# Scores from the edge features, computed in the first of two message phases

## The chip, the cores and the metric

The kernel runs on one core of a Trainium2 chip. The time is the device time of one execution in microseconds, shown as the median of several runs. A profiled execution gives, besides, when each instruction ran on each engine: PE (matrix products), DVE (vector work), ACT (activations and copies), POOL (here mostly gathers from memory, issued as indirect DMAs), and SP, which only issues DMAs.

## The reference, cut to what matters

The reference is a chain of four graph layers and four feed-forward layers over 3125 nodes with 256 features and 50000 edges sorted by destination. The change touches two graph layers.

Layer 0 adds up, for each node, transformed rows of the sources of its edges; layer 1 adds up products of embedding rows with a linear map of 64 edge features:

```
msg = transformed[rel_type, src] * norm                       # layer 0
W = (edge_feats @ W_dist + b_dist) * cut[:, None]             # layer 1
msgs = embed_table[node_z][senders] * W
agg = segment_sum(msgs, receivers)
```

Layer 2 is an attention over edges, whose logit has a part that depends on the edge features alone:

```
concat_z = concatenate([z[edge_src], z[edge_dst], w], axis=-1)   # w: edge features, 64 wide
e = leaky_relu(concat_z @ W_att.T)[:, 0]
```

The last 64 weights of `W_att`, times `w`, give one number for each edge: the "score from the edge features". It depends on inputs only, so a kernel can compute it at any time before layer 2.

## The kernel before, in words

The kernel starts with three pieces of work that share one hand-written order (`manual_schedule`: every engine executes its instructions in the order in which the program issues them).

**The first phase** (`stage_one`, L777 to 903). A short lead computes 24 `chunk`s. A chunk (L618) is one 128x512 piece of the table `tabt` of node rows, transformed for 16 relations; every fourth chunk SP writes 1 MB of it (L630). Then a loop over k from 0 to 195 (L880) does layer 1's sums. Every second step, `four` (L861) multiplies edge features by `wd` on PE into the PSUM tiles `pw` (three of them, filled with the bias by ACT, L858) and DVE multiplies the result by gathered embedding rows into `mt` (L871). Each step also does one more chunk until all 200 are done (k = 175), and lets POOL gather rows for a pair twelve steps ahead (`fetch_rows`, L810). Once in four steps come a feature load on SP (L851), the one-hot matrix on DVE (L825, L827), and `add_up` (L829): PE sums a group of edges, ACT copies it to `p_out` (L837), SP writes it out (L839 and L842). Four steps are called a round of the first phase here. In the remaining room, L900 takes one step of a background generator `bg` for each odd k. There `bg` is `ranks` (L1180), which finds where each node's edges begin; it has 25 yields.

**The second phase** (`stage_two`, L908 to 1176). Its loop has 49 groups of eight slots, 392 slots. Eight slots are a round of the second phase. Each round gathers eight tiles of `tabt` rows with POOL and adds up a group for layer 0 with `add_up`. As soon as a block of nodes has its sums, a `Flow` (L1109) takes two node tiles through the feed-forward layer 0, layer 1's output and the inputs of layer 2, spread over the next slots; three flows overlap, and each fetches its sums by gathers `p` on POOL (L927). Every second slot (`BG_EVERY`, L109) `between` (L1143) takes a step of a second background generator: first `by_degree` (L1273), which sorts the nodes by degree (37 yields), then `records` (L1352). From slot 60, zeros for later tables are written by SP in odd slots (L713).

`records` does four products for the attention weights (L1358), then the scores: 100 steps, each with one load of four edges for each of 125 partitions (`part`, L1367), three steps ahead of its use, a multiplication by the weights `a3` (L1377) and a sum over the 64 features into `rect` (L1378). Then it writes the pairs (source, score) to memory (L1384), reads them back in windows by node (`window`, L1389, 25 gathers on POOL), and masks them into `srcI` and `ewF` (L1401 to 1407).

Scores have four buffers (`b_at`), in the pool `sh` that both phases share. A score load's issue on SP thus waits for the sum of the step before, and it stands in SP's order behind whatever was issued earlier.

Of the kernel before, what the change touches and what calls it, by code (L numbers as in the profile page):

```python
# [9 lines left out]
F32 = mybir.dt.float32  # L10
# [3 lines left out]
OP = mybir.AluOpType  # L14
# [5 lines left out]
P = 128  # L20
# [4 lines left out]
D = 256  # L25
E = 50000
EP = 125
ET = 400
# [84 lines left out]
def tile_gnn_ffn(ctx: ExitStack, tc: tile.TileContext, a: dict, out: bass.AP):  # L113
# [7 lines left out]
    @contextmanager  # L121
    def psums(**bufs):
        with tc.tile_pool(name="psum", bufs=1, space=PSUM) as p:
            before = dict(banks)
            banks["pool"], banks["bufs"] = p, bufs
            yield
            banks.update(before)

    def ps(tag, shape):
        return banks["pool"].tile(shape, F32, name=tag, tag=tag, bufs=banks["bufs"][tag])  # L130
# [11 lines left out]
    def bcast(src, n, pool, name):  # L142

        t = pool.tile([P, n], F32, name=name)
        nc.sync.dma_start(t, bass.AP(tensor=src.tensor, offset=src.offset, ap=[[0, P], [1, n]]))
        return t
# [38 lines left out]
    wfa = per.tile([P, 2, ZW], F32, name="wfa")  # L185
# [198 lines left out]
    wb = w1st.enter_context(tc.tile_pool(name="wb", bufs=1))  # L384
    stt = nc.vector.scalar_tensor_tensor
# [22 lines left out]
    junk = pp.tile([EP, ET], F32, name="fl_junk")  # L408
# [48 lines left out]
    with tc.If(uns > 0):  # L457

        rec = dram.tile([E, RW], F32, name="rec")
        with tc.tile_pool(name="srt", bufs=1) as ep, tc.tile_pool(name="srt2", bufs=2) as eb, \  # L460
# [23 lines left out]
            for b in range(ET // BT):  # L484
# [10 lines left out]
                junk = eb.tile([EP, P], F32, name="s_junk")  # L495
                for i in range(BT):
# [5 lines left out]
                                                   op1=OP.mult, accum_out=before[:, 0, i : i + 1])  # L502
                    nc.vector.scalar_tensor_tensor(junk[:, :EP], row[:EP, e], dstf[:, j : j + 1], lower[:EP, :EP],
                                                   op0=OP.is_equal, op1=OP.mult, accum_out=before[:, 1, i : i + 1])
# [37 lines left out]
    def tp(width):  # L542
        return flatb()[:, :width]
# [233 lines left out]
    def stage_one():  # L777
# [24 lines left out]

        sh = w1st.enter_context(tc.tile_pool(name="sh", bufs=2))
        w = {}
        bg, loads = ranks(sh), late_weights(sh, w)
        pairs = NW // 2
        rows, feats, hots = {}, {}, {}
        at = {"rows": 0, "feats": 0, "chunk": LEAD}
# [35 lines left out]
        with tc.tile_pool(name="ea", bufs=1) as ea, psums(t=2, pw=3, agg=1, w=2):  # L844

            def fetch_feats():
                g = at["feats"]
                if g < NG:
                    at["feats"] += 1
                    feats[g] = ea.tile([P, 4 * P], F32, name="f", bufs=F_BUFS)  # L850
                    nc.sync.dma_start(feats[g], a["attr_2"][:, 4 * P * g : 4 * P * (g + 1)])  # L851

            mults, biased = {}, []

            def bias():

                pw = ps("pw", [P, 2, D])
                nc.scalar.copy(pw, bd.unsqueeze(1).to_broadcast([P, 2, D]))  # L858
                biased.append(pw)

            def four(k):  # L861

                g = k // 4
                for h in range(2):
                    for b in range(2):
                        o, half = (k % 4 + h) * P, slice(64 * b, 64 * b + 64)
                        nc.tensor.matmul(biased[b][:, h, :], feats[g][half, o : o + P], wd[half, :], start=False,
                                         stop=True, skip_group_check=True)
                for b in range(2):
                    m = mults[k + b] = ea.tile([P, 2, D], F32, name="mt", bufs=8)  # L870
                    nc.vector.tensor_tensor(m, biased.pop(0), rows.pop(k + b), op=OP.mult)  # L871

            for _ in range(F_BUFS - 1):
                fetch_feats()
            for _ in range(G_PAIRS):
                fetch_rows()
            make_hots(0, cutW)
            bias()
            bias()
            for k in range(pairs):  # L880
                g = k // 4
                if k % 4 == 0:
                    fetch_feats()
                if k % 2 == 0:
                    four(k)
                if at["chunk"] == 8 * NT:
                    next(loads, None)
                else:
                    chunk(next(chunks), ea)
                    at["chunk"] += 1  # L890
                    next(norms, None)
                if k % 2 == 0 and k + 2 < pairs:
                    bias()
                    bias()
                fetch_rows()
                if k % 4 == 1 and g:
                    add_up(g - 1, [mults.pop(4 * (g - 1) + j) for j in range(4)], part1)
                if k % 4 == 2:
                    make_hots(g + 1, cutW)
                if k % 2:  # L900
                    next(bg, None)
            add_up(NG - 1, [mults.pop(4 * (NG - 1) + j) for j in range(4)], part1)
            assert next(bg, None) is None and next(loads, None) is None
# [274 lines left out]
    begI_of = []  # L1178
# [92 lines left out]
    kept = {}  # L1271
# [77 lines left out]
        nc.vector.tensor_copy(begI, begR)  # L1349
        begI_of.append(begI)  # L1350

    def records(sh, w):  # L1352

        begI = begI_of[0]
        for i in range(2):
            for k in range(2):
                junk = sh.tile([P, D], F32, name="w_junk", bufs=1)
                stt(junk, wfa[:, k, :D], 1.0, w[f"aw{i}"], op0=OP.mult, op1=OP.mult, accum_out=wfa[:, k, D + i : D + i + 1])  # L1358
            yield

        a3 = bcast(a["L2_gnn_W_att"][:, 2 * D :], 64, wb, "b_a3")
        attr = a["edge_attr_64"].rearrange("(p t) d -> p t d", p=EP)
        rect = wb.tile([EP, ET, 2], F32, name="b_rect")
        nc.vector.tensor_copy(rect[:, :, 0], srcf)
        ats = {}

        def part(b):  # L1367
            if b < ET:
                ats[b] = sh.tile([EP, AB, 64], F32, name="b_at", bufs=4)
                nc.sync.dma_start(ats[b], attr[:, b : b + AB, :])  # L1370

        for b in range(0, 3 * AB, AB):
            part(b)
            yield
        for b in range(0, ET, AB):
            old = ats.pop(b)
            nc.vector.tensor_tensor(old, old, a3[:EP].unsqueeze(1).to_broadcast([EP, AB, 64]), op=OP.mult)  # L1377
            nc.vector.tensor_reduce(rect[:, b : b + AB, 1], old, axis=AX.X, op=OP.add)  # L1378
            part(b + 3 * AB)
            yield  # L1380

        nc.vector.tensor_sub(ews, ews, rect[:, :, 1])
        stt(rect[:, :, 1], ews, unsorted[:EP, :], rect[:, :, 1], op0=OP.mult, op1=OP.add)
        nc.sync.dma_start(rec2[:E, :].rearrange("(p t) w -> p t w", p=EP), rect)  # L1384
        yield

        ws = {}

        def window(t):  # L1389
            ws[t] = sh.tile([P, 32, 2], F32, name="k_w", bufs=3)  # L1390
            gather(ws[t][:, : RND[t], :].rearrange("p r w -> p (r w)"), rec2, begI[:, t : t + 1])

        window(0)
        window(1)
        for t in range(NT):
            n, s, w = RND[t], slice(OFF[t], OFF[t + 1]), ws.pop(t)
            if t + 2 < NT:
                window(t + 2)
            yield
            mk = sh.tile([P, 32], F32, name="k_mk")  # L1400
            nc.vector.tensor_scalar(mk[:, :n], iota_f[:, :n], degR[:, t : t + 1], None, op0=OP.is_lt)  # L1401
            sf = sh.tile([P, 32], F32, name="k_sf")
            stt(sf[:, :n], w[:, :n, 0], idF[:, t : t + 1], mk[:, :n], op0=OP.subtract, op1=OP.mult)
            nc.vector.tensor_scalar(srcI[:, s], sf[:, :n], idF[:, t : t + 1], None, op0=OP.add)
            nc.vector.tensor_tensor(ewF[:, s], w[:, :n, 1], mk[:, :n], op=OP.mult)
            nc.vector.tensor_scalar(mk[:, :n], mk[:, :n], BIG, -BIG, op0=OP.mult, op1=OP.add)
            nc.vector.tensor_add(ewF[:, s], ewF[:, s], mk[:, :n])

        for t in range(NT):
            nc.gpsimd.memset(rndF[:, t : t + 1], float(RND[t]))  # L1410
        mo = wb.tile([P, NT], F32, name="k_mo")
        mx = wb.tile([P, 1], F32, name="k_mx")
        nc.vector.tensor_sub(mo, degR, rndF)
        nc.vector.tensor_reduce(mx, mo, axis=AX.X, op=OP.max)
        pk = tp(P)
        nc.tensor.transpose(pk[:1], mx, ident)
        m0 = wb.tile([1, 1], F32, name="k_m0")
        nc.vector.tensor_reduce(m0, pk[:1], axis=AX.X, op=OP.max)
        nc.vector.tensor_scalar_max(m0, m0, 0.0)
        nc.vector.tensor_copy(more_i, m0)  # L1420
        yield

    stage_one()
    order.close()
    w1st.close()
# [23 lines left out]
    with tc.tile_pool(name="f1", bufs=1) as fp, tc.tile_pool(name="f1b", bufs=2) as fb, psums(mm=3, y=3, tp=2):  # L1449
# [17 lines left out]
        junk = fp.tile([P, NT], F32, name="f_junk")  # L1467
# [12 lines left out]
        for sh in range(28, -1, -4):  # L1480
# [3 lines left out]
            if sh < 28:  # L1484
# [8 lines left out]
                                    accum_out=c1)  # L1493
# [16 lines left out]
        with tc.If(tie > 0):  # L1510

            with tc.tile_pool(name="f1t", bufs=1) as tp_:
# [12 lines left out]
                for t in range(NT):  # L1525
                    w_ = wtb[:, t : t + 1]
                    nc.vector.tensor_scalar(less, row[:, :N], w_, None, op0=OP.is_gt, op1=OP.add,
                                            accum_out=cn[:, t, 0:1])
# [1010 lines left out]
```

## Time and profile before

| what | value |
|---|---|
| median of 3 runs | 3418.66 us (3414.97 to 3419.67) |
| the profiled execution | 3418.41 us, span 3416.7 us |
| mean granted clock of PE | 0.787 |
| busy: PE, DVE, ACT, POOL | 2240.7, 1678.1, 898.8, 1999.7 us |
| DMA: score loads | 100 of 125.0 KB, issued from 771.7 to 1103.6 us |
| DMA: table writes of the first phase | 50 of 1024.0 KB |
| DMA: feature loads, sum writes | 49 of 256.0 KB, 98 of 256.0 KB |

Busy time is a sum over the whole program. The two phases with which this text deals lie in the first 1320 us or so: layer 1's sums run from 106 to 650 us, the second phase's loop from there to about 1315 us. What limits one of them can be read only from windows of that time, and from the order of an engine's instructions: an engine that waits keeps all that stands behind it waiting. A number such as "4.66 <-ACT p_out L837" behind an instruction is the idle time of its engine before it, and what ended that.

### The profile page before, as it was taken

The numbers are of one execution on the slowest core, as the hardware profiler recorded it, in microseconds if no ns is written. First come the engines' busy times: TensorE is split into PE (matmuls) and PEld (weight loads), VectorE is DVE, ScalarE is ACT, GpSimd is POOL, SyncE is SP. The second block draws the span as 40 slices with busy tenths as digits, with TensorE's granted clock in tenths as the row PEclk, the third lists the DMA queues.
The fourth block names the chain that finished last, engine by engine and source line by source line (L and its number), as shares of the span: only waits on it lengthen the run. The fifth ranks groups of instructions, "written<-read, shape, count | busy, mean of one in ns | idle before, by whom it ended". The sixth has DMA issues, their size and how long they took to land. (4 is left out here: it accounts for less than half of the span.)

```text
span 3416.7 us, 36379 instructions
## 1 busy us (share of the span) xinstructions
PE 2240.7 (66%) x10325; PEld 1557.2 (46%) x10325; DVE 1678.1 (49%) x6067; ACT 898.8 (26%) x2016; POOL 1999.7 (59%) x2265
## 2 busy tenths in 40 slices
PE   4689999777888779849322585877711212259993
PEld 1334444345666557637211373756511112237672
DVE  2343333557787766533365565566723333366211
ACT  1334545312233223312110131323300000024341
POOL 3677777766666671011577777764467777732433
PEclk9889999758999889959655696888755555559997
DMA  7577777857775452031243585876233333325562
GB/s 238 183 229 245 254 253 251 255 135 228 235 235 177 111 144 80 31 130 50 80 111 104 158 262 176 266 257 188 95 90 106 105 105 106 105 76 165 166 217 81
DMA packets 246803, 553.65 MB, mean 162 GB/s; under 512 B 49584, under 2 KB 131251, under 8 KB 240174
## 3 DMA queue, kind: packets, MB, share of 16 engines
q0 software_dynamic: 103296, 283.74, 27.8%
q1 hardware_dynamic: 137624, 261.43, 23.6%
q10 hardware_dynamic: 5654, 5.88, 0.6%
q8 instruction: 90, 1.47, 0.2%
q14 instruction: 139, 1.14, 0.1%
HBM read 394.00 MB, written 156.83 MB: 161 GB/s over the span
## 5 line engine op out<-in xcount | busy, mean ns | idle before, releaser
L153 POOL DMA_INDIRECT g<-tabe,e_src x392 | 371.2, 947 | 196.2 <-issue 97.2
L153 POOL DMA_INDIRECT g_rows<-tab,srcI x413 | 402.4, 974 | 126.9 <-issue 104.8
L153 POOL DMA_INDIRECT g_row<-tab,srcI x413 | 390.6, 946 | 131.6 <-issue 119.8
L153 POOL DMA_INDIRECT g<-tabt,e_code x392 | 377.9, 964 | 151.1 <-issue 79.5
L625 PE MATMUL t<-w_big,n_xt 128*128 128x512 f32 x800 | 378.7, 619 | 0.5 <-ACT n_xt L613 0.5
L2386 DVE TENSOR_TENSOR ACC<-ACC,g_row 128x256 f32<-128x256 f32 x413 | 175.8, 426 | 341.4 <-DMA g_row<-tab,srcI 341.3
L1638 PE MATMUL tp<-ident,ACC 128*128 128x128 f32 x50 | 16.6, 435 | 420.4 <-DVE ACC L2386 420.4
L871 DVE TENSOR_TENSOR mt<-pw,g 128x512 f32<-128x512 f32 x196 | 126.7, 686 | 257.0 <-ACT p_out L837 145.6
L1970 PE MATMUL mm<-ro_xt,ro_w 128*128 128x192 f32 (+3 forms) x928 | 232.2, 401 | 28.9 <-ACT ro_h L2051 21.4
L1974 PE MATMUL y<-ro_w,ro_h 128*96 128x256 f32 (+2 forms) x1040 | 243.7, 388 | 1.5 <-ACT ro_h L2051 1.5
L625 PEld LDWEIGHTS t<-w_big,n_xt 128*128 128x128 f32 x800 | 148.8, 195 | 185.7 <-issue 184.1
L1018 PE MATMUL w<-xt,w_big 128*128 128x256 f32 (+1 forms) x832 | 214.2, 399 | 0.0
L2261 DVE SCALAR_TENSOR_TENSOR ACC<-g_rows,g_e,ACC 128x256 f32<-128x256 f32 x413 | 201.2, 487 | 13.4
L1970 PEld LDWEIGHTS mm<-ro_xt,ro_w 128*128 128x128 f32 x928 | 170.2, 205 | 73.3 <-ACT ro_h L2051 27.4
L157 POOL DMA_INDIRECT xg<-XX,ro_pos x100 | 100.8, 1008 | 174.8 <-issue 72.5
L1638 PEld LDWEIGHTS tp<-ident,ACC 128*128 128x128 f32 x50 | 7.2, 203 | 428.1 <-issue 353.2
L1974 PEld LDWEIGHTS y<-ro_w,ro_h 128*96 128x96 f32 (+2 forms) x1040 | 181.7, 180 | 44.1 <-ACT ro_h L2051 1.9
L1027 PE MATMUL w<-w_big,b_h 128*128 128x256 f32 x800 | 198.9, 387 | 1.6 <-DVE n_x L1029 1.6
L628 ACT COPY n_tst<-t 128x512 f32<-128x512 f32 x200 | 117.2, 586 | 266.7 <-PE t L625 239.7
L153 POOL DMA_INDIRECT ro_g<-yg,ro_back x100 | 99.4, 994 | 137.3 <-issue 67.4
L1018 PEld LDWEIGHTS w<-xt,w_big 128*128 128x128 f32 x832 | 162.7, 209 | 27.2 <-issue 4.9
L1027 PEld LDWEIGHTS w<-w_big,b_h 128*128 128x128 f32 x800 | 154.0, 195 | 24.2 <-DVE n_x L1029 2.0
(579 smaller groups left out, 4349.8 us busy)
## 6 DMA issues: line engine op xcount, KB each, us to landing
tabt<-n_tst SPq DMA_DIRECT2D x50, 1024.0 KB
ro_w<-in_L_ffn_blocks SPq DMA_DIRECT2D x58, 514.0 KB
ro_w<-in_L_ffn_blocks SPq DMA_DIRECT2D x58, 512.0 KB
part<-p_out SPq DMA_DIRECT2D x98, 256.0 KB
xg<-zero SPq DMA_DIRECT2D x78, 200.0 KB
f<-in_attr SPq DMA_DIRECT2D x49, 256.0 KB
b_at<-in_edge_attr SPq DMA_DIRECT2D x100, 125.0 KB
tabr<-v SPq DMA_DIRECT2D x11, 770.0 KB
```

The source lines that it names most:

```text
L153: return nc.gpsimd.indirect_dma_start(out=dst, out_offset=None, in_=table, in_offset=bass.IndirectOffsetOnAxis(ap=idx, axis=0))
L157: return nc.gpsimd.indirect_dma_start(out=table, out_offset=bass.IndirectOffsetOnAxis(ap=idx, axis=0), in_=src, in_offset=None)
L625: nc.tensor.matmul(pt, xt_of[t][:, k, :], wrel[:, k, 2 * i : 2 * i + 2, :].rearrange("p r d -> p (r d)"), start=(k == 0), stop=(k == 1))
L628: nc.scalar.copy(stage[0][:, o : o + 2 * D], pt)
L871: nc.vector.tensor_tensor(m, biased.pop(0), rows.pop(k + b), op=OP.mult)
L1018: nc.tensor.matmul(ph, w["01"][:, e, k, i * P : (i + 1) * P], xt[:, k, : n * h], start=(k == 0), stop=(k == 1))
L1027: nc.tensor.matmul(py, last[:, k, i * h : (i + 1) * h], w["02"][:, e - 1, k, :], start=(k == 0), stop=(k == 1))
L1638: nc.tensor.transpose(pt[:, k, :m], src[:, k * P : (k + 1) * P], ident[:m, :m])
L1970: nc.tensor.matmul(ph, w[:, o : o + P], xt[:, k, :], start=(k == 0), stop=(k == 1))
L1974: nc.tensor.matmul(py, h[:, i, s], w[:, i * D : (i + 1) * D], start=(i == 0), stop=(i == self.fc - 1))
L2261: stt(u, g[:, r, :D], e[:, r0 + r : r0 + r + 1], u, op0=OP.mult, op1=OP.add)
L2386: nc.vector.tensor_tensor(u, u, rows.pop(r), op=OP.max)
```

## The change

The part of `records` that computes the scores becomes a generator of its own, `scores`, with one yield for each of the three first loads and one for each of the 100 steps. It is appended to `ranks` in the first phase's background. Because the first phase would take too few steps with one for every odd k, from k = 56 on each k takes one. `records` finds the scores ready in `kept["rect"]`.

```diff
-        bg, loads = ranks(sh), late_weights(sh, w)
+        bg, loads = (step for part in (ranks(sh), scores(sh)) for step in part), late_weights(sh, w)
...
-                if k % 2:
+                if k % 2 or k >= 56:
                     next(bg, None)
...
-    def records(sh, w):
-
-        begI = begI_of[0]
-        for i in range(2):
-            for k in range(2):
-                junk = sh.tile([P, D], F32, name="w_junk", bufs=1)
-                stt(junk, wfa[:, k, :D], 1.0, w[f"aw{i}"], op0=OP.mult, op1=OP.mult, accum_out=wfa[:, k, D + i : D + i + 1])
-            yield
+    def scores(sh):
 
         a3 = bcast(a["L2_gnn_W_att"][:, 2 * D :], 64, wb, "b_a3")
         attr = a["edge_attr_64"].rearrange("(p t) d -> p t d", p=EP)
-        rect = wb.tile([EP, ET, 2], F32, name="b_rect")
+        rect = kept["rect"] = wb.tile([EP, ET, 2], F32, name="b_rect")
         nc.vector.tensor_copy(rect[:, :, 0], srcf)
         ats = {}
...
             nc.vector.tensor_tensor(old, old, a3[:EP].unsqueeze(1).to_broadcast([EP, AB, 64]), op=OP.mult)
             nc.vector.tensor_reduce(rect[:, b : b + AB, 1], old, axis=AX.X, op=OP.add)
             part(b + 3 * AB)
+            yield
+
+    def records(sh, w):
+
+        begI, rect = begI_of[0], kept["rect"]
+        for i in range(2):
+            for k in range(2):
+                junk = sh.tile([P, D], F32, name="w_junk", bufs=1)
+                stt(junk, wfa[:, k, :D], 1.0, w[f"aw{i}"], op0=OP.mult, op1=OP.mult, accum_out=wfa[:, k, D + i : D + i + 1])
             yield
 
         nc.vector.tensor_sub(ews, ews, rect[:, :, 1])
```

So the 100 loads and 200 DVE instructions of the scores are issued between k = 51 and k = 155 of the first phase, and `records`, which followed them, runs in the second phase right behind `by_degree`.

## The prediction

> **What bounds the kernel now.** I read the busy times by stretch first, then the timeline of one round of the first phase, the tile of the score loads, the ends of the second phase's rounds, and last the trace's DMA packets. The stretches (columns: busy us and instructions of PE, PEld, DVE, ACT and POOL, then granted clock, DMA share, GB/s):
>
> ```profile
> 300.00:600.00 300.00, 300.00 (x1396) 139.32 (x1392) 95.41 (x172) 151.16 (x285) 215.43 (x228) 1.00 0.77 252
> 840.00:1028.00 188.00, 162.19 (x867) 122.08 (x860) 147.69 (x551) 59.02 (x136) 121.54 (x126) 0.91 0.73 234
> 1028.00:1110.00 82.00, 73.00 (x377) 55.66 (x376) 63.60 (x240) 27.74 (x62) 53.17 (x55) 0.92 0.57 175
> 1121.00:1245.00 124.00, 89.24 (x437) 66.43 (x438) 82.94 (x380) 31.38 (x73) 87.87 (x115) 0.85 0.43 117
> 1245.00:1315.00 70.00, 64.57 (x367) 50.19 (x367) 46.31 (x196) 25.84 (x61) 40.02 (x42) 0.98 0.50 144
> ```
>
> The first phase (row one) is bound by PE: never idle at clock 1.00, DVE 32% busy. The second phase (rows two to five) has no full engine; DVE is 78% busy where the scores run. DVE in a round of the first phase (four steps k):
>
> ```profile
> 406.16 1.29 DVE L871 TENSOR_TENSOR mt<-pw,g 128x512 f32<-128x512 f32 x2 [4.66 <-ACT p_out L837]
> 407.37 0.42 DVE L825 TENSOR_TENSOR s<-iota_f,e_low 128x256 f32<-128x256 f32 x1
> 407.81 0.43 DVE L827 TENSOR_TENSOR s<-s,e_cut 128x256 f32<-128x256 f32 x1
> 410.86 1.29 DVE L871 TENSOR_TENSOR mt<-pw,g 128x512 f32<-128x512 f32 x2 [2.61 <-PE pw L867]
> 416.58 1.29 DVE L871 TENSOR_TENSOR mt<-pw,g 128x512 f32<-128x512 f32 x2 [4.44 <-ACT p_out L837]
> ```
>
> The round is 416.58 - 406.16 = 10.42 us, with 4.44 + 2.61 = 7.05 us in which DVE waits for PE. The score step that moves:
>
> ```profile
> L1370 SPq DMA_DIRECT2D b_at<-in_edge_attr x100: 257/275/2237, 771.7 to 1103.6; - x100
> L1377 DVE TENSOR_TENSOR b_at<-b_at,b_a x100: 391/418/487, 782.5 to 1115.9; 125x256 f32<-125x256 f32 x100
> L1378 DVE TENSOR_REDUCE b_rect<-b_at x100: 419/420/422, 783.1 to 1116.3; 125x4 f32<-125x256 f32 x100
> ```
>
> And ends of the second phase's rounds (eight slots; round 9 ends at 775.95, 35 at 1121.53, 42 at 1244.72, 48 at 1314.55):
>
> ```profile
> 775.95 0.59 ACT L837 COPY p_out<-agg 128x512 f32<-128x512 f32 x1 [0.68 <-PE agg L834]
> ...
> 1121.53 0.56 ACT L837 COPY p_out<-agg 128x512 f32<-128x512 f32 x1
> ...
> 1244.72 0.59 ACT L837 COPY p_out<-agg 128x512 f32<-128x512 f32 x1 [0.74 <-PE agg L834]
> ...
> 1314.55 0.59 ACT L837 COPY p_out<-agg 128x512 f32<-128x512 f32 x1 [0.73 <-PE agg L834]
> ```
>
> So a round takes 345.6/26 = 13.3 us beside scores, 123.2/7 = 17.6 us beside the windows (the gathers k_w), and 69.8/6 = 11.64 us with neither.
>
> **DMA engines.** The trace counts a DMA's semaphore up engine by engine. Of each zero write between 900 and 1000 us eleven engines report first, close together (most within 4 us), a twelfth is in between, and four come late, mostly 7 to 10 us after the issue. The score loads (125 partitions) get only about five such reports after landing begins, the sum writes of L839 (4x32 rows) four. So these DMAs do not use all engines, and the slow ones are the same few. Their load, with the median packet times of the trace (1024 B 46 ns, 1600 B 67, 2048 B 84, 4096 B 159, 8192 B 309), score packets spread over five engines, sum writes over four, all else over sixteen: in stretches of 40 us from 776 to 1096 it is 1.02, 0.94, 1.00, 1.03, 1.00, 1.00, 0.94, 0.89 of the time. These engines were full for 240 us while the mean DMA share stood at 0.73.
>
> **Removed from the second phase.** 100 steps of 0.418 + 0.420 us on DVE, one in two slots (3.35 us a round), 100 SP issues of 0.275 us, 12.8 MB of loads, and a 0.36 us copy. Records, its 25 window gathers on POOL and 25 memsets come 204 slots sooner: rounds 10 to 16, beside the early flows. Windows cost POOL four more gathers a round: (8 + 1 + 4) x 1.25 us (a gather 0.95 plus 0.30 to the next) = 16.3, near the 17.6 seen, so I keep 7 x 17.6 = 123.2 us, which also holds the 11.3 us that POOL waits for the records' write. Rounds 9 to 48 last 1314.55 - 775.95 = 538.6 us. After: 123.2 + 32 x 11.64 = 496 us, a gain of 43; I take 40 for meeting early flows. Bounds: 32 rounds at POOL's own 9 x 1.25 = 11.25 us gain 55; at 12.4 us, if PE's chains through DVE and ACT stay the limit, 19. The zero writes that now run beside clean rounds cost nothing: the rounds beside scores were no slower with them (13.3 against 13.5 us), and without scores the few engines have room.
>
> **Added to the first phase.** Score step i runs at k = 56 + i, one a step until k = 155: 25 rounds, with three loads ahead at k = 51, 53, 55. The b_rect copy and the a3 broadcast load come once, under the same idle.
> DVE: 4 x 0.84 = 3.35 us into 7.05 us idle. Two steps behind one mt leave 4.44 - 1.68 = 2.8 us, the two behind the one-hots 2.61 - 1.68 = 0.9: nothing, if the loads are there. The cover is PE's ten microseconds of work.
> SP: four issues more (1.1 us) beside four others (1.7 us) in 10.42 us: nothing. They stand in order behind the table write (waits for ACT n_tst L628) and the sum write (waits for p_out), so a load leaves when its round has come that far.
> POOL: nothing is issued; a gather waits for mt to free its rows, twelve pairs ahead, so its lateness is covered.
> The few DMA engines, per round now: table write 8 x 309 = 2.47 us, feature load 8 x 84 = 0.67, eight gathers 16 x 159 = 2.54, sum write 32 x 84 = 2.69, small ones 0.1: 8.5 of 10.42 us. The scores add 4 x 25 x 46 ns = 4.6 us. Together 13.1 us. At most 1.03 full was seen, so a round cannot be shorter than 12.7; at 0.99 it is 13.2. DVE runs in order: a score's multiply that waits for its load holds the next mt, ACT's bias copies wait for mt (three pw banks), PE's pw for those. Three loads ahead bridge no lasting shortage. So 25 x (13.2 - 10.42) = 70 us. Bounds (PE is full, so no gain is to be had here): nothing, as for the mean load (252 GB/s + 4 x 128,000 B/10.42 us = 301 GB/s, and the trace held 350 GB/s at 10 to 30 us); and with the mean packet times of 300 to 600 us (queueing included: 10.4 + 5.05 = 15.4 us) 125 us. I take 70, nearest to the stretch from 776 to 1028, which has these same score loads, sum writes and gathers on full engines.
> PE's clock: 0.91 at 86% busy in row two. PE's 10.42 us at 0.85 are 12.3, still under 13.2: nothing more; it is in the upper bound.
>
> Rule against row: the Trainium skill, DMA: Bandwidth & Descriptors, section Bandwidth, gives about 358 GB/s per core as the limit for transfers with HBM. By it 301 GB/s fit, the 70 us vanish, and the sum would be 3418.4 - 40 = 3378. The row speaks against taking one limit for all sixteen engines: 234 GB/s went with few engines full.
>
> **Sum** against the profiled execution (3418.4 us, span 3416.7, within 0.3 us of the median 3418.66): + 70 - 40 = + 30, so 3448 us.
>
> **Rivals.**
> A, the loads are hidden and the change gains. For it: 7.05 us of idle DVE, a mean share of 0.77, peaks of 350 GB/s, a lead of three steps (7.8 us). Against: score loads that DVE waited for had been issued 8.3 to 11.8 us before. It decides if the round stays under 10.42 + 40/25 = 12.0 us, a load of 13.1/12.0 = 1.09 on the few engines, where 1.03 was the most seen. Cost 0 to 20, gain 40 to 55: 3363 to 3398.
> B, cost and gain cancel: round at 11.8 to 12.3 us with a gain of 40 to 45: 3408 to 3425.
> C, worse than counted: loads late in bursts, PE falling to half clock in the gaps (0.64 at 71% busy between 700 and 800), rounds of 14.3 to 15.4 us: + 97 to 125, less 20 to 40: 3475 to 3523.
> That the scores stay where they were is excluded: the changed program issues all 100 between the first phase's mt.
>
> **How the numbers follow.** Few engines full 0.66 (own range 3428 to 3475), A 0.18, B 0.07, C 0.09. A measurement tells 0.2% (6.8 us) from nothing: faster 0.18, same 0.07, slower 0.75. The range from 3392 to 3490 leaves out most of A's better half and C's worse half.
>
> **What would show it.** Right: between about 300 and 620 us rounds near 13.2 us instead of 10.42, PE under 85% busy, DVE's score multiply (now L1370) waiting for b_at for 60 us or more; the first phase's last round some 70 us later; then rounds of 17.6 us from round 10 and under 12 us from round 17, p_out of round 48 near 1345 us; all after that as before. Wrong: rounds of 10.4 us there (A), or rounds of 13 us in the second phase without scores, which would mean that DVE was not what they shared.

## The result and the profile after

The changed kernel takes 3443.09 us (median of 6 runs, 3440.36 to 3444.44) beside 3419.16 us for the kernel before in the same comparison: 1.0070 of it, 95% interval 1.0057 to 1.0083, so it is slower by 24 us. Its profiled execution took 3440.36 us, with a span of 3438.6. Some of the later comparisons ran about a fifth slower as a whole, the kernel before included (4051 to 4131 us at a granted clock of 0.74 to 0.75, instead of some 3419 us at 0.78 to 0.79); why is open, and no reading rests on them.

Busy times by stretch of the changed kernel (columns as before: PE, PEld, DVE, ACT, POOL, granted clock, DMA share, GB/s):

```profile
360.00:600.00 240.00, 217.74 (x885) 98.29 (x886) 117.54 (x252) 94.43 (x181) 137.44 (x146) 0.98 0.70 240
...
1000.00:1100.00 100.00, 92.65 (x518) 72.15 (x516) 66.53 (x271) 36.10 (x83) 74.55 (x78) 0.98 0.75 233
```

In the first phase PE is no longer without gaps, and DMA moves *less* per microsecond than before (240 against 252 GB/s), although the score loads came in. In the second phase DVE has gone from 78% to 67%. The ends of rounds show what that did to each phase. First rounds 14 and 38 of the first phase in the kernel before:

```profile
320.83 0.59 ACT L837 COPY p_out<-agg 128x512 f32<-128x512 f32 x1 [0.39 <-PE agg L834]
...
573.57 0.59 ACT L837 COPY p_out<-agg 128x512 f32<-128x512 f32 x1 [0.39 <-PE agg L834]
```

Then the changed kernel (rounds 14, 19, 38 and the last, 48, of the first phase, then 9, 16, 35 and 48 of the second):

```profile
320.38 0.60 ACT L837 COPY p_out<-agg 128x512 f32<-128x512 f32 x1
...
385.99 0.57 ACT L837 COPY p_out<-agg 128x512 f32<-128x512 f32 x1
...
638.51 0.60 ACT L837 COPY p_out<-agg 128x512 f32<-128x512 f32 x1
...
724.49 0.59 ACT L837 COPY p_out<-agg 128x512 f32<-128x512 f32 x1 [10.74 <-DMA part<-p_out]
...
841.90 0.59 ACT L837 COPY p_out<-agg 128x512 f32<-128x512 f32 x1 [0.68 <-DMA xg<-zero]
...
962.74 0.59 ACT L837 COPY p_out<-agg 128x512 f32<-128x512 f32 x1 [1.60 <-PE agg L834]
...
1184.12 0.56 ACT L837 COPY p_out<-agg 128x512 f32<-128x512 f32 x1
...
1337.40 0.59 ACT L837 COPY p_out<-agg 128x512 f32<-128x512 f32 x1 [0.97 <-PE agg L834]
```

| stretch | before | after |
|---|---|---|
| a round of the first phase (14 to 38) | 252.74/24 = 10.53 us | 318.13/24 = 13.26 us |
| end of the first phase's last round | 660.1 us | 724.5 us |
| second phase, rounds 9 to 48 | 538.6 us | 495.5 us |
| rounds with windows (35 to 42 before, 9 to 16 after) | 17.6 us | 17.3 us |
| rounds 16 to 35 | 13.4 us (with scores) | 11.65 us (nothing beside) |
| end of round 48 | 1314.6 us | 1337.4 us |

The first phase loses 64 to 66 us and the second gains 43. After the second phase's loop the kernels run alike: the spans differ by 21.9 us, the loops' ends by 22.9.

How the loss reaches PE is told by the changed kernel's waits between 360 and 600 us (us in total, times, longest):

```profile
DVE b_at L1370 <- DMA b_at<-in_edge_attr: 118.0, 71, 3.2
POOL g L153 <- DVE mt L871: 69.3, 36, 3.6
...
ACT pw L858 <- DVE mt L871: 59.9, 34, 3.5
PEld pw L867 <- ACT pw L858: 48.9, 51, 2.1
```

DVE's multiply waits for its load, mt stands behind it, ACT's bias copy waits for mt, PE's pw for the copy. Over the whole run DVE waited 164.7 us for score loads, in 98 of 100 steps; before, in the second phase, 17.5 us in 9. The same in one round of DVE's timeline:

```profile
428.29 0.42 DVE L1370 TENSOR_TENSOR b_at<-b_at,b_a 125x256 f32<-125x256 f32 x1 [2.95 <-DMA b_at<-in_edge_attr]
428.75 0.42 DVE L1371 TENSOR_REDUCE b_rect<-b_at 125x4 f32<-125x256 f32 x1
429.42 0.43 DVE L1370 TENSOR_TENSOR b_at<-b_at,b_a 125x256 f32<-125x256 f32 x1 [0.25 <-DMA b_at<-in_edge_attr]
429.88 0.42 DVE L1371 TENSOR_REDUCE b_rect<-b_at 125x4 f32<-125x256 f32 x1
430.22 1.28 DVE L871 TENSOR_TENSOR mt<-pw,g 128x512 f32<-128x512 f32 x2
```

mt now follows a late score step without a gap; before, it had waited 2.6 to 4.7 us for PE.

### The profile page after: what moved, and what is told of

Same layout as the page of the kernel before. It is cut to its first block, busy times and chain, and to the rows that moved or that the text cites. A ratio compares the mean times of both kernels' runs of the same rounds, so it can differ in the third digit from the quotient of the medians.

```text
span 3438.6 us, 36411 instructions
## 1 busy us (share of the span) xinstructions
PE 2254.0 (66%) x10325; PEld 1559.6 (45%) x10325; DVE 1687.1 (49%) x6067; ACT 895.3 (26%) x2016; POOL 1997.9 (58%) x2265
## 5 line engine op out<-in xcount | busy, mean ns | idle before, releaser
L2263 DVE SCALAR_TENSOR_TENSOR ACC<-g_rows,g_e,ACC 128x256 f32<-128x256 f32 x413 | 201.2, 487 | 13.4
L867 PE MATMUL pw<-w_d,f 64*128 64x256 f32 x784 | 156.0, 423 | 78.3 <-ACT pw L858 66.4
L1018 PE MATMUL w<-xt,w_big 128*128 128x256 f32 (+1 forms) x832 | 204.3, 386 | 0.0
```

The lines of the kernel that those rows point to most:

```text
L1018: nc.tensor.matmul(ph, w["01"][:, e, k, i * P : (i + 1) * P], xt[:, k, : n * h], start=(k == 0), stop=(k == 1))
L2263: stt(u, g[:, r, :D], e[:, r0 + r : r0 + r + 1], u, op0=OP.mult, op1=OP.add)
```

## The experiments

The theory: a load of 125 partitions runs on five DMA engines and the sum write of L839 on four of the same, so these engines are full while the rest are not. Its rivals: the lead of three loads is too short for a longer latency; SP cannot issue that much, or the DMA system as a whole is full. And for the second phase: was its gain from DVE's relief, or from the engines'?

**Spread the score loads** (changed kernel):

```diff
-                nc.sync.dma_start(ats[b], attr[:, b : b + AB, :])
+                for lo, hi in ((0, 112), (112, EP)):
+                    nc.sync.dma_start(ats[b][lo:hi], attr[lo:hi, b : b + AB, :])
```

> Each score load is issued as two, of 112 and of 13 partitions, so that its packets can be spread over 16 and 13 engines instead of five; bytes, packets, lead and DVE work stay. Few full engines (my theory): the fullest engine then has 8.5 + 4 x 8 x 0.046 = 10.0 us of packets in a round of the first phase, PE's 10.42 us bind again, rounds of 10.4 to 10.8 us, total 3443 - 65 = 3378 us (3370 to 3386). SP's issue or the DMA system as a whole is the limit (after the change SP's issues last up to 3.7 us): four more issues in a round and the same bytes, rounds of 13.3 us or more, total 3443 or more. The lead is too short for the latency: rounds shorten only as far as each load lands sooner, somewhere between 10.5 and 13.

Measured: 3382.72 us beside 3421.55, ratio 0.9881 (0.9855 to 0.9907). Rounds of the first phase take 252.75/24 = 10.53 us, the number of the kernel before. Its rounds 14 and 38, and its stretch from 360 to 600 us:

```profile
320.51 0.59 ACT L837 COPY p_out<-agg 128x512 f32<-128x512 f32 x1 [0.39 <-PE agg L834]
...
573.26 0.59 ACT L837 COPY p_out<-agg 128x512 f32<-128x512 f32 x1 [0.39 <-PE agg L834]
```

```profile
360.00:600.00 240.00, 240.00 (x1125) 111.37 (x1123) 140.19 (x296) 121.73 (x230) 175.35 (x183) 1.00 0.88 294
```

PE is without gaps again, with the same bytes to move, one issue more for each step, and DMA at 294 GB/s. So neither SP's issues nor the whole of DMA were the limit. What the scores cost in the first phase is nothing, once their loads are spread, and this kernel keeps the second phase's gain (494.2 us for rounds 9 to 48). It is faster than both kernels.

**Spread the sum writes instead** (changed kernel; the score loads stay on five engines):

```diff
-            nc.sync.dma_start(v[:, :8, :].rearrange("l (j h) d -> j l (h d)", h=2), o)
+            for j in range(4):
+                nc.sync.dma_start(v[:, 2 * j : 2 * j + 2, :].rearrange("l h d -> l (h d)"), o[32 * j : 32 * j + 32, :])
```

> The score loads stay as the change has them; instead the sum write of L839 (4 x 32 rows) is issued as four writes of 32 rows, which can use 16 engines each. Few full engines: 8.5 - 2.69 + 0.67 + 4.6 = 11.1 us on the fullest engines, rounds of 11.0 to 11.5 us where the scores are, total near 3443 - 25 x 2.1 = 3391 us. SP's issue or all of the DMA system: three more issues in a round, 13.3 us or more, 3443 or more. Lead too short: about 13.3 us, since the score loads are issued as before.

Measured: 3402.53 us (one run), rounds of 275.78/24 = 11.49 us (rounds 14 and 38 shown):

```profile
321.87 0.59 ACT L837 COPY p_out<-agg 128x512 f32<-128x512 f32 x1 [0.39 <-PE agg L834]
...
597.65 0.60 ACT L837 COPY p_out<-agg 128x512 f32<-128x512 f32 x1
```

The score loads were issued as in the changed kernel, with as short a lead, and yet 1.8 us of each round went. The account by packets said 11.1; the fullest engines were at 0.96 by it. The total is above the 3391 expected, chiefly because the round came out at the upper end.

**A longer lead** (changed kernel):

```diff
-                ats[b] = sh.tile([EP, AB, 64], F32, name="b_at", bufs=4)
+                ats[b] = sh.tile([EP, AB, 64], F32, name="b_at", bufs=7)
...
-        for b in range(0, 3 * AB, AB):
+        for b in range(0, 6 * AB, AB):
             part(b)
-            yield
+            if b % (2 * AB):
+                yield
...
-            part(b + 3 * AB)
+            part(b + 6 * AB)
```

> The score loads run six steps ahead (seven buffers) instead of three. Lead too short for the latency: the loads are in time, rounds of 10.4 to 11 us, total 3378 to 3392 us. Few full engines, or SP's issue: a longer lead bridges no lasting shortage, rounds stay at 13.0 to 13.4 us, total 3436 to 3446 us.

Measured: 3442.88 us (one run), rounds of 13.34 us; DVE waits 165.5 us for loads, as with a lead of three (164.7). So it is a shortage of throughput, not of lead.

**The same spread in the kernel before** (the first edit, at its L1370):

> The kernel before, with its score loads (in the second phase) issued as two of 112 and 13 partitions. It asks what held the rounds of the second phase beside the scores at 13.3 us. Few full engines there too (1.00 full by packet times from 776 to 1028 us): rounds of 11.7 to 12.3 us, total 3419 - 26 x 1.3 = 3385 us (3379 to 3394). DVE's 3.35 us of score work a round in the chains of PE and ACT: rounds stay at 13.3 us, total 3415 to 3421 us.

Measured: 3411.72 us, ratio 0.9970 (0.9959 to 0.9981). Neither expectation held fully. The early rounds, 9 to 16, shorten from 12.9 to 11.8 us, but rounds 16 to 35 stay at 13.48 us (13.43 before):

```profile
777.01 0.59 ACT L837 COPY p_out<-agg 128x512 f32<-128x512 f32 x1 [0.68 <-PE agg L834]
...
859.85 0.59 ACT L837 COPY p_out<-agg 128x512 f32<-128x512 f32 x1 [1.60 <-PE agg L834]
...
1116.01 0.56 ACT L837 COPY p_out<-agg 128x512 f32<-128x512 f32 x1
```

So in the second phase the full engines cost some 7.5 us in the early rounds, and something else held the later ones.

**The two halves of a score step, each in another phase** (changed kernel: the loads stay in the first phase and nothing reads them; the DVE instructions go to the second phase, where they were, and multiply the first four edges each time, so the scores are other numbers). The edit is cut at each "...":

```diff
@@ scores
-            nc.vector.tensor_tensor(old, old, a3[:EP]..., op=OP.mult)
-            nc.vector.tensor_reduce(rect[:, b : b + AB, 1], old, axis=AX.X, op=OP.add)
             part(b + 3 * AB)
...
@@ records, before the records are written
+        only = wb.tile([EP, AB, 64], F32, name="b_only")
...
+        for b in range(0, ET, AB):
+            old = sh.tile([EP, AB, 64], F32, name="b_at", bufs=4)
+            nc.vector.tensor_tensor(old, only, a3[:EP]..., op=OP.mult)
+            nc.vector.tensor_reduce(rect[:, b : b + AB, 1], old, axis=AX.X, op=OP.add)
+            yield
```

> One kernel that takes the score step apart and puts its halves into different phases: the 100 score loads in the first phase, on five engines, read by nothing, and the 200 DVE instructions in the second phase, where the kernel before had them, multiplying the first four edges each time (so the scores are other numbers). First phase, rounds 14 to 38: if DVE's wait for a load in front of mt carries the loads' lateness to PE, 10.5 us; if the full engines and SP's order do so by themselves, 12.7 to 13.3 us (I expect this). Second phase, rounds 16 to 35: if DVE's instructions made the rounds beside the scores 13.4 us, 13.0 to 13.5 us (I expect this); if the loads did, 11.6 to 12.2 us. Total by my expectations 3419 + 60 = 3479 us (3465 to 3490); by the other two 3419 - 35 = 3384 us.

> The same kernel once more (score loads in the first phase, read by nothing; DVE's score instructions in the second, on the first four edges), beside a kernel before that takes some 3420 us again, if this chip gives that. First phase, rounds 14 to 38: 10.5 us if only DVE's wait carries the loads' lateness to PE, 12.7 to 13.3 us if the full engines and SP's order do so by themselves (I expect this). Second phase, rounds 16 to 35: 13.0 to 13.5 us if DVE's instructions made the rounds beside the scores (I expect this), 11.6 to 12.2 us if the loads did. Total by my expectations 3465 to 3490 us.

The first of these took 4066.78 us beside 4070.74 for the kernel before, and nothing is read from it. The second took 3472.04 us (one run) beside 3419.15. Rounds 14 to 38 of the first phase: 308.36/24 = 12.85 us. Rounds 16 to 35 of the second: 13.40 us. Both as expected. First the waits, between 360 and 600 us, then the ends of rounds 14, 19, 38 and 48 of the first phase and of rounds 9, 16, 35 and 48 of the second:

```profile
ACT n_tst L628 <- DMA tabt<-n_tst: 83.4, 15, 7.5
...
DVE mt L871 <- PE pw L867: 64.9, 18, 5.4
```

```profile
319.61 0.59 ACT L837 COPY p_out<-agg 128x512 f32<-128x512 f32 x1 [0.39 <-PE agg L834]
...
372.87 0.58 ACT L837 COPY p_out<-agg 128x512 f32<-128x512 f32 x1
...
627.97 0.61 ACT L837 COPY p_out<-agg 128x512 f32<-128x512 f32 x1
...
723.69 0.59 ACT L837 COPY p_out<-agg 128x512 f32<-128x512 f32 x1 [11.45 <-DMA part<-p_out]
...
839.50 0.59 ACT L837 COPY p_out<-agg 128x512 f32<-128x512 f32 x1 [0.68 <-PE agg L834]
...
921.21 0.59 ACT L837 COPY p_out<-agg 128x512 f32<-128x512 f32 x1 [1.60 <-PE agg L834]
...
1175.74 0.56 ACT L837 COPY p_out<-agg 128x512 f32<-128x512 f32 x1
...
1366.68 0.59 ACT L837 COPY p_out<-agg 128x512 f32<-128x512 f32 x1 [1.05 <-PE agg L834]
```

With nobody reading the score loads, DVE waits for PE again, but the loads still hold the phase: ACT cannot refill the table's staging buffers, because table writes have not landed. The last engine of such a write reports 11.8 to 13.8 us after the issue, against 5.7 to 6.8 in the kernel before.

The mean of 12.85 us hides two parts. The first five rounds still take 53.26/5 = 10.65 us; from round 19 to 38 a round takes 255.10/19 = 13.43 us, no less than in the changed kernel (252.52/19 = 13.29). The last round ends 63.6 us later than in the kernel before, against 64.4 us in the changed kernel; some 7 of the 63.6 come in the last three rounds, after the loads, and why is not shown. So the full engines, with SP's order, slow a round as much without DVE's wait; with that wait the slowing begins five rounds sooner. That the buffers of the table and the sums bridge the first five rounds is our reading, and no run tests it.

In the second phase DVE's 3.35 us of score instructions alone, without their loads, make a later round of 13.4 us; the gain of 1.75 us a round was DVE's. The early rounds, 9 to 16, take 11.67 us without the loads, much as with the loads spread (11.83). Rounds 9 to 48 take 527.2 us here, between the 538.6 of the kernel before and the 495.5 of the changed one: of the gain of 43 us about 11 went with the loads and about 32 with DVE's instructions.

**Both spreads together, and the halves taken alone.** Nothing is read from these runs, beside which the kernel before took 4051 to 4131 us.

> Both spreads together: score loads as 112 and 13 partitions, sum writes as four of 32 rows. In the first phase PE binds already with the first spread alone (rounds of 10.53 us), so nothing is to be had there; in the second phase the sums land sooner for the gathers that wait for them, but POOL's 11.25 us bind the clean rounds of 11.6. Expected 3376 to 3384 us, the same as with the score loads spread alone (3382.7). A rival that holds the few engines for the limit of the clean rounds too expects 11.3 us there and 3370 or less.

Measured: 4104.42 us beside 4131.24, ratio 0.9948 (0.9929 to 0.9967).

> The kernel after the change with the scores' 200 DVE instructions left out (the scores are filled with other numbers): the loads into b_at stay, on five engines, and nothing reads them, so that only their four buffers hold them back. It asks how the loads reach PE. If DVE's wait for a load, which stands in front of mt, carries it: rounds back at 10.5 us, total 3443 - 65 = 3378 us. If the engines and SP's one order do (table, feature and sum DMAs share the full engines and stand behind the score loads on SP): rounds of 12.7 to 13.3 us, total 3430 to 3443 us. I expect the second.

Measured: 4098.92 us (one run) beside 4131.24, rounds of 12.68 us in the first phase.

> The kernel before with 99 of the 100 score loads left out: every score step multiplies the first four edges again, so DVE's 200 instructions stay where they were, in the second phase. If DVE's instructions in its order hold the rounds beside the scores: 13.0 to 13.5 us, total 3409 to 3421. If the loads (SP's order, engines) do: 11.6 to 12.2 us, total 3380 to 3392.

> Again the kernel before with 99 of the 100 score loads left out and DVE's 200 score instructions kept in the second phase (every step multiplies the first four edges). If DVE's instructions in its order hold the rounds beside the scores: 13.0 to 13.5 us there, total 3409 to 3421 us beside 3419. If the loads (SP's order, the few engines) do: 11.6 to 12.2 us, total 3380 to 3392 us.

Measured: 4108.69 us beside 4131.24, and 4112.73 beside 4107.60; rounds 16 to 35 of 16.1 us both times.

> The kernel before with the scores' 200 DVE instructions left out (the scores are filled with other numbers) and the 100 loads kept in the second phase. If DVE's instructions hold the rounds beside the scores: 11.6 to 12.2 us, total 3380 to 3392 us. If the loads do: 13.0 to 13.5 us, total 3409 to 3421 us.

> Again the kernel before with the scores' 200 DVE instructions left out (the scores are filled with other numbers) and the 100 loads kept in the second phase, since in the last comparison every kernel, the one before too, took some 700 us more. If DVE's instructions hold the rounds beside the scores: 11.6 to 12.2 us there, total 3380 to 3392 us beside 3419. If the loads do: 13.0 to 13.5 us, total 3409 to 3421 us.

Measured: 4102.59 us beside 4131.24, and 4036.57 beside 4051.10; rounds 16 to 35 of 15.7 us.

In the four of these runs that have no score loads in the first phase, its rounds took 12.4 to 12.5 us, so that they could not tell 10.5 from 13. Their questions were answered by the last run of the halves, except two: whether spreading the sum writes as well brings more than spreading the loads alone, and whether the loads alone, without DVE's instructions, would have held the second phase's later rounds.

## Why the prediction was right

**Few engines, the term of 70 us: right, and shown.** Forecast rounds of 13.2 us, measured 13.26. By the packet times the fullest engines were at 0.98 of the time between 360 and 620 us. The term measures 65 us instead of 70 (rounds 14 to 38 take 318.13 - 252.74 = 65.4 us more). The round before was 10.53 us on the mean and not the 10.42 of the one that was read, which makes 2.7 us over 25 rounds, and only 24 of the 25 rounds were lengthened in full (the one from 13 to 14 took 11.5 us). Spreading one of the two kinds of DMA took away 1.8 us of a round, spreading the other 2.7, with the bytes unchanged.

The table writes, which use all sixteen engines, show the full ones directly. Between 360 and 600 us of the changed kernel the twelfth engine of such a write reports 7.2 us after the issue and the sixteenth 13.0 us after it, the length of a round; in the kernel before it was 5.1 and 6.3 us (medians of 17 writes each).

The Trainium skill, DMA: Bandwidth & Descriptors, says why it is five and four engines (section "Why a DMA increments its semaphore by 16 and not by 1"): a DMA issued by SP is split over the largest number up to 16 that divides the slowest dimension of both its sides, on the lowest-numbered engines. The numbers agree in the trace: of each of the 72 score loads in that stretch five engines report, of each of the 19 sum writes of L839 four, and of a split load up to 16 and 13. No trace here names the engines; that the loads and the sum writes share theirs follows from the round getting shorter when either was spread.

That page's section Bandwidth gives about 358 GB/s as the limit, which neither kernel reached in this stretch. By that limit alone the 70 us would have vanished, and they did not: 240 GB/s was all that went, and 294 GB/s fitted as soon as the loads were spread.

**The way to PE: as foretold, but not the only one.** DVE's in-order wait, mt, bias, pw appear in the waits as foretold. That the loads hold the phase just as much when nothing reads them (13.43 us a round from round 19 on) was not in the prediction; there ACT waits for the table writes, and PE for ACT. **The DVE, SP and POOL terms** of the first phase, set to nothing, were nothing by themselves: with the loads spread the round is 10.53 us. But SP's issues, counted at 2.8 us a round, took 10.3 us of a round in the changed kernel.

**The gain of 40 us: right.** 43.1 us measured; clean rounds at 11.65 against 11.64, windows at 17.3 against 17.6. The later rounds' gain came from DVE's instructions, as the halves show; that these act through the chains of PE and ACT is argued and not shown. The few engines, at 0.89 to 1.03 by the same account from 776 to 1096 us, held only the early rounds there: an engine that is full need not be the one that binds.

**The sum:** + 65 - 43 = + 22 by the profile, + 24 by the medians, forecast + 30. **Wrong in detail:** PE was to be under 85% busy and was 91% at clock 0.98. From 360 to 600 us it did 885 matmuls, 79% of the 1125 of the kernel with spread loads, but one was busy for 0.246 us on the mean instead of 0.213, and why is not shown. The reserve for a lower clock was not needed, nor the upper bound from mean packet times (15.4 us a round, where 13.26 came).

**Rivals:** A (hidden, a gain) fell, and its total came true once the loads were spread (3382.7 us). B and C fell.

## What to carry to other kernels

A mean DMA share does not show the fullest engine: 0.70 stood beside 0.98 here. Count, for each DMA of a phase, over how many engines it is split, and add up packet time engine by engine before moving a load into a phase that "has bandwidth"; 125 partitions cost here what 112 + 13 did not. Work that is free on its own engine can still bring transfers along that are not, and here, where the engines run in order, one late transfer held the work behind it on DVE or on ACT.

## What the runs showed of the hardware that was not expected

SP's issues got longer when the few engines were full. In the first phase of the kernel before, then of the changed kernel (SP's timeline: start, length):

```profile
406.25 0.47 SPq L842 DMA_DIRECT2D part<-p_out  x1
...
410.35 0.33 SPq L630 DMA_DIRECT2D tabt<-n_tst  x1
```

```profile
432.87 2.28 SPq L630 DMA_DIRECT2D tabt<-n_tst  x1
...
440.64 3.48 SPq L842 DMA_DIRECT2D part<-p_out  x1
```

From 360 to 620 us SP spent 202.7 of 260 us in issues, against 48.9 of 300 before (300 to 600 us); with the loads spread it was 124.3 of 250 (330 to 580 us), with twice as many issues for the loads. The mean issue went from 0.43 to 1.29 us, and back to 0.46. Long issues were here a sign of full engines, not a cost of issuing.
